# An attention layer in three-part float32: later column sums in the last image, a third form buffer and a shorter bias in the first, a reordered end

## The chip, the cores and the metric

The kernel runs on one core of one Trainium2 chip. The time is that of one execution of the whole program on the device, in microseconds (us). Before the change it was 2398.16 us, the median of three runs (2396.82 to 2399.83).

## The reference, cut to what matters

```python
# x: (4, 64, 64, 256); N = 64*64 = 4096, C = 256, C2 = 128
q = x @ Wq + bq          # (B, N, C2)
k = x @ Wk + bk          # (B, N, C2)
v = x @ Wv + bv          # (B, N, C)
pq, pk = q.reshape(B, C2, N), k.reshape(B, C2, N)
pv = v.reshape(B, C, N)
energy = einsum('bcn,bcm->bnm', pq, pk)      # 4096 x 4096 for each image
attention = softmax(energy, axis=-1)
out = einsum('bcm,bnm->bcn', pv, attention)  # 256 x 4096
result = gamma * out.reshape(x.shape) + x
```

Four images, each with its own 4096 by 4096 attention. The softmax is taken without subtracting a maximum; the kernel checks at its end that all sums lie in a safe range and has a second, general path behind a branch for the case that they do not.

## The kernel before, in words

Every float32 operand of a large product is split into forms: an upper part h, a lower part l and a third, d, which carries the correction, and each product is made of the three pairs. The forms are stored in the type that TensorE (PE) streams at one column per cycle. ScalarE (ACT) makes h, VectorE (DVE) makes l and d. So each large product is three matmuls on PE, one activation on ACT and two operations on DVE.

Work is staged like this:

- **Start** (lines 116 to 140 and 548 to 574). Weights and bias are loaded, Wq with Wk by the ACT queue, Wv by SyncE's. `weights(w)` scales a weight tile on ACT (line 160) and makes its forms with `split` (line 152 on ACT, 155 on DVE); w = 0 is q and k together, w = 1 is v. The bias of q and k is split too: an upper form on ACT (line 560) and a lower on DVE (line 563), each over 128 rows at 1/128 of its value, since `biased` (line 243) adds them by products with a tile of ones. The first tile of x is transposed (line 198), split (`x_forms`, lines 209, 211, 213) and multiplied.
- **First image's projections** (loop at line 575, 16 iterations i). An iteration issues, on PE: the f = 0 and 1 products of q and k (`products(0, i, 0, (0, 1))`, eight matmuls, line 229), those of v (eight), then for i + 1 the f = 2 products of q and k (four), the bias (four), the f = 2 products of v (four), and the transposes for i + 2 (four, line 198). On ACT, in this order: the h form of q and k (line 268), the h form of v (line 152), `seed_qk` for i + 1 (line 251), the h form of x for i + 2 (line 209), `seed_v` for i + 1 (line 260, two). The seeds scale a PSUM bank in place between the f = 2 products and the others. On DVE: two forms of q and k (line 271), two of v (line 155), two of x (211, 213). `qk_forms` takes its tile f from a ring of two buffers (tag "pf"), and `store` (line 290) sends it to DRAM by four DMAs on GpSimd's (POOL's) queue: k and q, for each of two halves. Parts of the first two attention steps are laid into iterations 7 to 12, and `load_q` and `load_k` stand at iterations 4, 5, 6, 8 and 11 on POOL's queue, behind the stores.
- **Attention steps** (loop at line 613). 512 steps n: 128 per image, in groups of NU = 16; t = n % 16 is the place in a group. A group is 512 rows of queries, a step 256 keys. Step n issues `cross(n+2)` (two products, line 318, each then scaled by ACT, line 319, in its PSUM tile; there are two such tiles), `attend(n, 0)` (six products into banks a0 and b0, line 378), `energy(n+2)` (four products, line 333, and two exponentials on ACT, line 336), `attend(n, 1)` (six, into a1 and b1). `upper` makes h of the exponentials on ACT (line 342), `halves` adds them to the running sum on DVE (line 351) and makes l and d (356, 358); in a group's last step it also adds the two halves of the sum (line 362). In steps of the first three images the next image's projections are woven in; the last image has attention alone.
- **End of a group.** At t = 15 `emptied(n, 0)` copies banks a0 and b0 to the tile o (ACT, line 392; o has one buffer) and `sum_forms` splits the sum (lines 404, 406). `emptied(n, 1)` copies a1 and b1 at t = 0 of the next group in the first three images and at t = 1 in the last (`late`). In the same step, behind it on PE, `sums` multiplies the column sums with a tile of ones (z, line 416, two products) and copies one row of z on ACT (line 417). In the last image z takes a bank that the second copy of line 392 has just emptied. `finish` then runs one piece a step from that step on: sums to DRAM and back, reciprocal (429), sum of the two parts of o (432), reciprocals spread over all rows by DMA, product (438), an accumulating DMA of x on POOL's queue (442) and the store on SyncE's (446).
- **The last group's end** (`finish_last`, line 453): attend(n, 0); zp, eight small products for the sums (459); reciprocal (463); spread (466); the range check (450, 451, 473); the d products of attend(n, 1); rp, the reciprocals on all rows (478); the rest of attend(n, 1); np (481). ACT copies b1 (482), then r (484). DVE ends with lines 485 to 492, two stores leave (488, 493), and `again` (494) is written for the branch.

Nothing reorders the instructions: each engine runs them in the order in which the code issues them.

Of the kernel before, what the change touches and what calls it, by code (L numbers as in the profile page):

```python
# [9 lines left out]
F32 = mybir.dt.float32  # L10
# [10 lines left out]
def kernel(  # L21
# [79 lines left out]
    with ExitStack() as fast:  # L101
# [45 lines left out]
                if next(pieces, StopIteration) is StopIteration:  # L147
                    active.remove(pieces)

        def split(h, l, d, y, scale=E):  # L150

            nc.scalar.activation(h, y, AF.Identity, scale=UPPER * scale)
            yield
            for t, f in ((d, 1.0 / scale + 1.0), (l, 1.0 / scale)):
                nc.vector.scalar_tensor_tensor(t, h.bitcast(F32), -f, y, ALU.mult, ALU.add)
                yield

        def weights(w):

            nc.scalar.mul(scaled[:, w], raw[:, w], E ** -(w + 1))  # L160
            yield from split(*(wf[:, w, f] for f in range(3)), scaled[:, w])

        def image(b):
            for g in range(NG):
# [73 lines left out]
        def biased(i):  # L238

            to = units[0, 0, i]  # L240
            for f in range(2):
                for s in range(2):
                    nc.tensor.matmul(  # L243
                        to[:, s, :], ones_r, bf[:, f, :], start=False, stop=False,
                        skip_group_check=True,
                    )

        def seed_qk(b, i):
            y = units[0, b, i]
# [13 lines left out]

        def qk_forms(b, i):
            y = units.pop((0, b, i))
            f = work.tile([P, 2, 3, C], F32R, tag="pf", name=f"f_{b}_{i}")
            h = f[:, :, 0, :]
            nc.scalar.activation(h, y, AF.Identity, scale=UPPER / 64)
            yield
            for j, s, op in ((1, -64.0, ALU.add), (2, 64.0 * (1.0 + E), ALU.subtract)):  # L270
                nc.vector.scalar_tensor_tensor(f[:, :, j, :], h.bitcast(F32), s, y, ALU.mult, op)  # L271
                yield
            for s in range(2):
                stores.append((kf[b, i // 2 + NU // 2 * s][:, i % 2], f[:, s, :, C2:]))
                stores.append((qd[b, i // NJ + NG // 2 * s][:, i % NJ], f[:, s, :, :C2]))
# [69 lines left out]
        def halves(n):  # L345
            if n >= B * STEPS:
                return
            x, h = units[n]
            if n % NU:
                s = now["s"]  # L350
                nc.vector.tensor_tensor(s, s, x, ALU.add)  # L351
            else:
                now["s"] = x
            ld = ppool.tile([P, 2, 2, NB], F32R, tag="ld", name=f"ld_{n}")
            l, d = ld[:, 0], ld[:, 1]
            nc.vector.tensor_tensor(l, x, h.bitcast(F32), ALU.subtract)  # L356

            nc.vector.scalar_tensor_tensor(  # L358
                d, h.bitcast(F32), 1.0 + E, x, ALU.mult, ALU.subtract
            )  # L360
            if n % NU == NU - 1:
                nc.vector.tensor_tensor(s[:, 0, :], s[:, 0, :], s[:, 1, :], ALU.add)
                now["sum"] = s
            units[n] = h, l, d

        def attend(n, j, order=(0, 1, 2)):
# [20 lines left out]
        def emptied(n, j, banks=None):  # L387

            if j == 0:
                now["o"] = work.tile([P, 2, 2, NB], F32, tag="o", name=f"o_{n // NU}", bufs=1)  # L390
            for c, scale in enumerate((gam2, gam1)):
                nc.scalar.activation(  # L392
                    now["o"][:, c, j, :],
                    banks[c] if banks else now["ab"[c], j],
                    AF.Identity,
                    scale=scale,
                )
# [55 lines left out]
        def finish_last(n, xr):  # L453

            b, g = B - 1, NG - 1
            attend(n, 0)
            zp = ps_e.tile([P, NJ], F32, tag="e", name="zp")
            for j in range(NJ):
                nc.tensor.matmul(
                    zp[:, j : j + 1], now["sum"][:, 0, j::NJ], ones[:, :1], start=True, stop=True  # L460
                )
            r4 = rall[:, B * NG - 1, :]
            nc.vector.reciprocal(r4, zp)
            work_ = ppool.tile([P, 2, NB], F32, tag="x", name="last")
            spread, ok = work_[:, 0].rearrange("p (q j) -> p q j", j=NJ), work_[:, 1, : B * NG * NJ]
            nc.vector.tensor_tensor(
                spread,
                ident.unsqueeze(2).to_broadcast([P, P, NJ]),
                r4.unsqueeze(1).to_broadcast([P, P, NJ]),
                ALU.mult,  # L470
            )
            inside(ok, rall.rearrange("p n j -> p (n j)"))
            nc.vector.tensor_reduce(zs, ok, AX.X, ALU.min)
            emptied(n, 0)
            o = now["o"]
            attend(n, 1, (2,))
            rp = ps_e.tile([P, NB], F32, tag="e", name="rp")
            nc.tensor.matmul(rp, ones, work_[:, 0], start=True, stop=True)
            attend(n, 1, (0, 1))
            np_ = ps_p.tile([P, 1], F32, tag="p0", name="np")  # L480
            nc.tensor.matmul(np_, ones, zs, start=True, stop=True)
            nc.scalar.activation(o[:, 1, 1, :], now["b", 1], AF.Identity, scale=gam1)
            r = work.tile([P, NB], F32, tag="r", name="r_last", bufs=1)
            nc.scalar.copy(r, rp)
            nc.vector.tensor_tensor(o[:, 0, 0, :], o[:, 0, 0, :], o[:, 1, 0, :], ALU.add)
            nc.vector.tensor_tensor(o[:, 0, 0, :], o[:, 0, 0, :], r, ALU.mult)
            nc.vector.tensor_tensor(xr[:, 0, :], xr[:, 0, :], o[:, 0, 0, :], ALU.add)
            nc.sync.dma_start(og[b, g][:, 0], xr[:, 0, :])
            nc.vector.tensor_tensor(o[:, 1, 1, :], o[:, 1, 1, :], r, ALU.mult)
            nc.vector.tensor_tensor(xr[:, 1, :], xr[:, 1, :], o[:, 1, 1, :], ALU.add)  # L490
            nc.vector.scalar_tensor_tensor(o[:, 0, 1, :], now["a", 1], gam2, r, ALU.mult, ALU.mult)
            nc.vector.tensor_tensor(xr[:, 1, :], xr[:, 1, :], o[:, 0, 1, :], ALU.add)
            nc.sync.dma_start(og[b, g][:, 1], xr[:, 1, :])
            nc.vector.tensor_scalar(again, np_, P - 0.5, None, ALU.is_lt)


        R = STEPS // NI
# [51 lines left out]
        now["turn"], now["banks"] = 0, [(ps_p, "p0"), (ps_p, "p1")]  # L549
        rings = cycle(now["banks"]), cycle([(ps_o, tag) for tag in ("a0", "a1", "b0", "b1")])  # L550
        image(0)
        for i in range(4):
            load_x(0, i)
        bf = work.tile([P, 3, KC, 2, P], F32R, tag="xf", name="bf", bufs=1)
        bf = bf[:, 0].rearrange("p k s a -> p k (s a)")
        transposed(0, 0)
        first = [weights(0), x_forms(0, 0), weights(1)]
        for pieces in first + first:
            next(pieces)
        nc.scalar.activation(bf[:, 0], bias, AF.Identity, scale=UPPER / P)  # L560
        for pieces in first:
            next(pieces)
        nc.vector.scalar_tensor_tensor(
            bf[:, 1], bias, 1.0 / P, bf[:, 0].bitcast(F32), ALU.mult, ALU.subtract
        )
        nc.gpsimd.tensor_scalar(bias, bias, REST, None, ALU.mult)
        products(0, 0, 0, (2,))
        products(0, 0, 1, (2,))
# [6 lines left out]
        for i in range(NI):  # L575
            products(0, i, 0, (0, 1))
            qk = qk_forms(0, i)
            next(qk)
            products(0, i, 1, (0, 1))
            vs = v_forms(0, i)  # L580
            next(vs)
            xs = iter(())
            if i + 1 < NI:
                products(0, i + 1, 0, (2,))
                biased(i + 1)
                seed_qk(0, i + 1)
                products(0, i + 1, 1, (2,))
            if i + 2 < NI:
                transposed(0, i + 2)
                xs = x_forms(0, i + 2)  # L590
                next(xs)
            if i + 1 < NI:
                seed_v(0, i + 1)
            load_x(0, i + 4)
            for pieces in (qk, vs, xs):
                for _ in pieces:
                    pass
            store()
            if i in (7, 10):
                cross(i // 9)  # L600
            elif i in (8, 11):
                energy(i // 9)
            elif i in (9, 12):
                upper(i // 10)
            elif i == 14:
                halves(0)
            if i == 4:
                load_q(0, 0)
            if i in (4, 5, 6):
                load_k(i - 4)  # L610
            elif i in (8, 11):
                load_k(3 + i // 9)
        for n in range(B * STEPS):
# [33 lines left out]
            else:  # L647
                upper(n + LOOK)
            step(p, "pe")
            if t == late and n > 1:  # L650
                sums(n - 1 - late)
                active.append(finish(n // NU - 1, now["o"], now["total"]))
            halves(n + 1)
            if turn:
# [232 lines left out]
```

## Time and profile before

| | |
|---|---|
| time, median of 3 runs | 2398.16 us (2396.82 to 2399.83) |
| profiled execution, its own time | 2397.88 us |
| its span | 2396.1 us |
| granted TensorE clock over the span | 0.996 |
| PE busy | 2355.5 us (98%), 11158 matmuls |
| DVE busy | 2135.3 us (89%) |
| ACT busy | 1882.2 us (79%) |
| POOL busy | 580.7 us (24%) |
| attention products (lines 318, 333, 378) on the chain that ended last | 87% |

A busy PE is the mean of overlapping records: a 512-column product lasts 0.39 us in its record but the next starts 0.227 us after it. In the timeline a row gives the start, the length, engine, line and operation, what is written and read, and in brackets how long the engine had been idle and what released it. Where several instructions of a group follow each other they are merged into one row with a count.

### The profile page before, as it was taken

To read this page: it belongs to the slowest core of one execution; us is meant where nothing else is said; L and a number is where in the kernel's file an instruction comes from. 1 tells how busy PE (TensorE), PEld (TensorE's weight loads), DVE (VectorE), ACT (ScalarE), POOL (GpSimd) and SP (SyncE) were. 2 spreads that over 40 slices of the span, in tenths; PEclk is the share of its full clock that TensorE was granted. 3 is DMA by queue.
4 is the path that set the end of the run, shared out by engine and by line. 5 is a ranking of instruction groups with operands and counts; after the bars stand their busy time and mean duration, and the time that the engine had idled before them with its cause. 6 is when DMAs were issued, how large, how long until landed. Compare 5 with 4: busy or idle time off the path is not lost.

```text
span 2396.1 us, 31995 instructions
## 1 busy us (share of the span) xinstructions
PE 2355.5 (98%) x11158; PEld 1967.6 (82%) x11158; DVE 2135.3 (89%) x2111; ACT 1882.2 (79%) x3093; POOL 580.7 (24%) x943
## 2 busy tenths in 40 slices
PE   8999999999999999999999999999999999999998
PEld 7888888888888888888888888888888787777776
DVE  6889999999999999999999999999998888888887
ACT  6777788887888887888877888878887777777775
POOL 5422222222322222222232222222223111111110
PEclk9999999999999999999999999999999999999999
DMA  9857666567896576566697665676669545445443
GB/s 216 177 139 199 169 165 171 144 174 183 262 274 163 147 187 178 157 166 156 164 342 220 159 175 142 175 188 156 167 175 337 134 128 128 126 111 129 114 124 88
DMA packets 243991, 413.83 MB, mean 173 GB/s; under 512 B 26031, under 2 KB 141487, under 8 KB 243822
## 3 DMA queue, kind: packets, MB, share of 16 engines
q0 software_dynamic: 203152, 368.77, 59.2%
q1 hardware_dynamic: 40126, 42.67, 5.7%
q8 instruction: 91, 1.49, 0.3%
q14 instruction: 78, 0.64, 0.1%
q10 hardware_dynamic: 544, 0.26, 0.0%
HBM read 306.64 MB, written 104.98 MB: 172 GB/s over the span
## 4 chain that ended last, share of the span: by engine, by line
PE 96%; ACT 2%; DVE 1%; DMA 1%; issue 0%; POOL 0%; SPq 0%; ACTq 0%; DVEq 0%
PE a L378 39%; PE b L378 19%; PE e L333 19%; PE e L318 10%; PE qv L229 7%; PE xt L198 1%; PE z L416 1%; ACT x L336 0%; ACT o L392 0%; DMA qd<-f 0%; ACT qv L260 0%; DMA raw<-in_L_conv_Wv_dram 0%; PE qv L243 0%; ACT xf L209 0%; DVE ld L358 0%
## 5 line engine op out<-in xcount | busy, mean ns | idle before, releaser
L336 ACT ACTIVATE x<-e 128x512 f32<-128x512 f32 x960 | 522.0, 596 | 301.7 <-PE e L333 295.4
L305 POOL DMA_DIRECT2D k<-kf x512 | 275.5, 538 | 1738.3 <-PE e L333 1678.3
L356 DVE TENSOR_TENSOR ld<-x,h 128x1024 fp32r<-128x1024 f32 x480 | 586.0, 1221 | 100.5 <-ACT h L342 55.8
L351 DVE TENSOR_TENSOR s<-s,x 128x1024 f32<-128x1024 f32 x480 | 586.5, 1222 | 99.7 <-ACT x L336 97.5
L378 PE MATMUL a<-h,v 128*128 128x512 f32 x2048 | 642.9, 395 | 0.0
L319 ACT ACTIVATE e<-e 128x512 f32<-128x512 f32 x1024 | 546.4, 572 | 119.7 <-PE e L318 119.3
L378 PE MATMUL b<-ld,v 128*128 128x512 f32 x2048 | 632.7, 390 | 1.7 <-DVE f L271 1.5
L378 PE MATMUL a<-ld,v 128*128 128x512 f32 x2048 | 633.8, 391 | 0.0
L358 DVE SCALAR_TENSOR_TENSOR ld<-h,x 128x1024 fp32r<-128x1024 f32 x480 | 584.7, 1218 | 0.0
L333 PE MATMUL e<-q,k 128*128 128x512 f32 x2048 | 547.7, 389 | 0.0
L342 ACT ACTIVATE h<-x 128x1024 fp32r<-128x1024 f32 x480 | 510.5, 1064 | 13.2
L378 PEld LDWEIGHTS b<-ld,v 128*128 128x128 f32 x2048 | 384.8, 188 | 84.6 <-issue 1.9
L378 PEld LDWEIGHTS a<-ld,v 128*128 128x128 f32 x2048 | 385.4, 188 | 83.4
L333 PEld LDWEIGHTS e<-q,k 128*128 128x128 f32 x2048 | 384.2, 188 | 79.7
L378 PEld LDWEIGHTS a<-h,v 128*128 128x128 f32 x2048 | 369.5, 189 | 70.6 <-ACT o L392 7.3
L318 PE MATMUL e<-q,k 128*128 128x512 f32 x1024 | 316.2, 390 | 0.0
L318 PEld LDWEIGHTS e<-q,k 128*128 128x128 f32 x1024 | 192.2, 188 | 40.8
L229 PEld LDWEIGHTS qv<-xf,wf 128*128 128x128 f32 x768 | 107.5, 191 | 17.9 <-ACT qv L260 8.0
L229 PE MATMUL qv<-xf,wf 128*128 128x256 f32 x768 | 114.5, 285 | 7.2 <-ACT qv L260 5.4
L229 PE MATMUL qv<-wf,xf 128*128 128x256 f32 x768 | 114.9, 286 | 3.6 <-DVE xf L211 1.9
L229 PEld LDWEIGHTS qv<-wf,xf 128*128 128x128 f32 x768 | 108.1, 192 | 12.7 <-ACT qv L251 2.6
L290 POOL DMA_DIRECT2D kf<-f x128 | 98.3, 768 | 29.1 <-DVE f L271 6.9
(84 smaller groups left out, 1230.4 us busy)
## 6 DMA issues: line engine op xcount, KB each, us to landing
k<-kf POOLq DMA_DIRECT2D x512, 384.0 KB, 3.6
vf<-vf POOLq DMA_DIRECT2D x48, 768.0 KB, 5.3
v<-vf POOLq DMA_DIRECT2D x48, 768.0 KB, 8.3
kf<-f POOLq DMA_DIRECT2D x128, 192.0 KB, 4.4
qd<-f POOLq DMA_DIRECT2D x128, 192.0 KB, 4.4
q<-qd POOLq DMA_DIRECT2D x32, 768.0 KB, 5.2
o<-in_x_dram POOLq DMA_DIRECT2D x31, 512.0 KB, 7.4
out_dram<-o SPq DMA_DIRECT2D x31, 512.0 KB
```

Of the source, the lines that this page charges most:

```text
L229: nc.tensor.matmul(to[:, s, :], left, right.rearrange("p s a -> p (s a)") if w else right, start=(f == 2 and s == k == 0), stop=(f == 1 an ...
L290: nc.gpsimd.dma_start(to, f)
L305: nc.gpsimd.dma_start(t, kf[b, u % NU])
L318: nc.tensor.matmul(e, *forms(n, i, 2), start=True, stop=False, skip_group_check=True)
L319: nc.scalar.mul(e, e, -REST)
L333: nc.tensor.matmul(e, *forms(n, i, f), start=False, stop=(f == 1), skip_group_check=True)
L336: nc.scalar.activation(x[:, i, :], e, AF.Exp, scale=(1.0 + E) ** 3 / E)
L342: nc.scalar.activation(h, units[n], AF.Identity, scale=UPPER)
L351: nc.vector.tensor_tensor(s, s, x, ALU.add)
L356: nc.vector.tensor_tensor(l, x, h.bitcast(F32), ALU.subtract)
L358: nc.vector.scalar_tensor_tensor(d, h.bitcast(F32), 1.0 + E, x, ALU.mult, ALU.subtract)
L378: nc.tensor.matmul(to, vall[:, t, f, i, j * P : (j + 1) * P], units[n][f][:, i, :], start=(t == 0 and i == 0 and f != 1), stop=(t == NU - ...
```

## The change

Five edits.

1. **Last image's column sums.** `sums` and the start of `finish` move from t = 1 to t = 2 in the last image (`t == 2 * late`); `emptied` stays. In the first three images (late = 0) nothing moves.
2. **Third buffer.** Every third `qk_forms` tile of the first image is a fixed tile f3, in a buffer of the q ring (tag "q", two buffers) that `load_q` does not use yet.
3. **seed_v earlier.** In the first image's loop `seed_v(0, i + 1)` is issued ahead of the transposes and the h form of x for i + 2. The order on ACT becomes h of q and k, h of v, seed_qk, seed_v (two), h of x.
4. **Bias and weights.** The bias is one product for each half, over 64 rows: a zero tile whose row 0 holds the upper form and row 32 the lower. `biased` issues two matmuls in place of four. The weights' scaling moves from ACT to DVE, and their h form reads the unscaled weights. In program order DVE gets the zero fill and both scalings ahead of all forms, and two one-row bias operations in place of one over 128 rows.
5. **The end.** In the last step the halves of the sum are added ahead of l and d. `finish_last` issues zp and the range check ahead of attend(n, 0), then rp and np, then all of attend(n, 1). ACT copies r ahead of b1. `again` is written ahead of the last products, and the second half is done in three DVE operations in place of four.

```diff
-        def split(h, l, d, y, scale=E):
+        def split(h, l, d, y):
...
         def weights(w):
-            nc.scalar.mul(scaled[:, w], raw[:, w], E ** -(w + 1))
-            yield from split(*(wf[:, w, f] for f in range(3)), scaled[:, w])
+            y, c = scaled[:, w], E ** -(w + 1)
+            nc.vector.tensor_scalar(y, raw[:, w], c, None, ALU.mult)
+            h, l, d = (wf[:, w, f] for f in range(3))
+            nc.scalar.activation(h, raw[:, w], AF.Identity, scale=UPPER * E * c)
+            yield
+            for t, f in ((d, 1.0 / E + 1.0), (l, 1.0 / E)):
+                nc.vector.scalar_tensor_tensor(t, h.bitcast(F32), -f, y, ALU.mult, ALU.add)
+                yield
...
         def biased(i):
-            for f in range(2):
-                for s in range(2):
-                    nc.tensor.matmul(
-                        to[:, s, :], ones_r, bf[:, f, :], start=False, stop=False,
-                        skip_group_check=True,
-                    )
+            for s in range(2):
+                nc.tensor.matmul(
+                    to[:, s, :], ones_r[:64], bf[:64], start=False, stop=False,
+                    skip_group_check=True,
+                )
...
         def qk_forms(b, i):
-            f = work.tile([P, 2, 3, C], F32R, tag="pf", name=f"f_{b}_{i}")
+            if b == 0 and i % 3 == 2:
+                f = f3
+            else:
+                f = work.tile([P, 2, 3, C], F32R, tag="pf", name=f"f_{b}_{i}")
...
         def halves(n):
+            def whole():
+                nc.vector.tensor_tensor(s[:, 0, :], s[:, 0, :], s[:, 1, :], ALU.add)
+                now["sum"] = s
+
+            if n == B * STEPS - 1:
+                whole()
...
-            if n % NU == NU - 1:
-                nc.vector.tensor_tensor(s[:, 0, :], s[:, 0, :], s[:, 1, :], ALU.add)
-                now["sum"] = s
+            if n % NU == NU - 1 and n < B * STEPS - 1:
+                whole()
...
         def finish_last(n, xr):
-            attend(n, 0)
             zp = ps_e.tile([P, NJ], F32, tag="e", name="zp")
...
             nc.vector.tensor_reduce(zs, ok, AX.X, ALU.min)
+            attend(n, 0)
             emptied(n, 0)
             o = now["o"]
-            attend(n, 1, (2,))
             rp = ps_e.tile([P, NB], F32, tag="e", name="rp")
             nc.tensor.matmul(rp, ones, work_[:, 0], start=True, stop=True)
-            attend(n, 1, (0, 1))
             np_ = ps_p.tile([P, 1], F32, tag="p0", name="np")
             nc.tensor.matmul(np_, ones, zs, start=True, stop=True)
-            nc.scalar.activation(o[:, 1, 1, :], now["b", 1], AF.Identity, scale=gam1)
+            attend(n, 1, (2, 0, 1))
             r = work.tile([P, NB], F32, tag="r", name="r_last", bufs=1)
             nc.scalar.copy(r, rp)
+            nc.scalar.activation(o[:, 1, 1, :], now["b", 1], AF.Identity, scale=gam1)
             nc.vector.tensor_tensor(o[:, 0, 0, :], o[:, 0, 0, :], o[:, 1, 0, :], ALU.add)
+            nc.vector.tensor_scalar(again, np_, P - 0.5, None, ALU.is_lt)
...
-            nc.vector.tensor_tensor(o[:, 1, 1, :], o[:, 1, 1, :], r, ALU.mult)
-            nc.vector.tensor_tensor(xr[:, 1, :], xr[:, 1, :], o[:, 1, 1, :], ALU.add)
-            nc.vector.scalar_tensor_tensor(o[:, 0, 1, :], now["a", 1], gam2, r, ALU.mult, ALU.mult)
-            nc.vector.tensor_tensor(xr[:, 1, :], xr[:, 1, :], o[:, 0, 1, :], ALU.add)
+            y = o[:, 1, 1, :]
+            nc.vector.scalar_tensor_tensor(y, now["a", 1], gam2, y, ALU.mult, ALU.add)
+            nc.vector.tensor_tensor(y, y, r, ALU.mult)
+            nc.vector.tensor_tensor(xr[:, 1, :], xr[:, 1, :], y, ALU.add)
             nc.sync.dma_start(og[b, g][:, 1], xr[:, 1, :])
-            nc.vector.tensor_scalar(again, np_, P - 0.5, None, ALU.is_lt)
...
         image(0)
+        f3 = work.tile([P, 2, 3, C], F32R, tag="q", name="f3")
...
-        bf = bf[:, 0].rearrange("p k s a -> p k (s a)")
+        bf, bh = (bf[:, 0, k].rearrange("p s a -> p (s a)") for k in range(KC))
+        nc.vector.tensor_scalar(bf[:64], zs[:64].to_broadcast([64, C]), 0.0, None, ALU.mult)
         transposed(0, 0)
...
-        nc.scalar.activation(bf[:, 0], bias, AF.Identity, scale=UPPER / P)
+        nc.scalar.activation(bh[:64], bias[:64], AF.Identity, scale=UPPER)
         for pieces in first:
             next(pieces)
-        nc.vector.scalar_tensor_tensor(
-            bf[:, 1], bias, 1.0 / P, bf[:, 0].bitcast(F32), ALU.mult, ALU.subtract
-        )
+        nc.vector.tensor_copy(bf[:1], bh[:1].bitcast(F32))
+        nc.vector.tensor_tensor(bf[32:33], bias[32:33], bh[32:33].bitcast(F32), ALU.subtract)
...
                 products(0, i + 1, 1, (2,))
+                seed_v(0, i + 1)
             if i + 2 < NI:
                 transposed(0, i + 2)
                 xs = x_forms(0, i + 2)
                 next(xs)
-            if i + 1 < NI:
-                seed_v(0, i + 1)
...
-            if t == late and n > 1:
-                sums(n - 1 - late)
+            if t == 2 * late and n > 2:
+                sums(n - 1 - 2 * late)
                 active.append(finish(n // NU - 1, now["o"], now["total"]))
```

More of the change, by code (lines that the diff above doesn't have):

```diff
@@ L148, in proceed @@
                     active.remove(pieces)
-        def split(h, l, d, y, scale=E):
-            nc.scalar.activation(h, y, AF.Identity, scale=UPPER * scale)
+        def split(h, l, d, y):
+            nc.scalar.activation(h, y, AF.Identity, scale=UPPER * E)
             yield
-            for t, f in ((d, 1.0 / scale + 1.0), (l, 1.0 / scale)):
+            for t, f in ((d, 1.0 / E + 1.0), (l, 1.0 / E)):
                 nc.vector.scalar_tensor_tensor(t, h.bitcast(F32), -f, y, ALU.mult, ALU.add)
@@ L158, in weights @@
         def weights(w):
-            nc.scalar.mul(scaled[:, w], raw[:, w], E ** -(w + 1))
-            yield from split(*(wf[:, w, f] for f in range(3)), scaled[:, w])
+            y, c = scaled[:, w], E ** -(w + 1)
[3 more added lines that the diff above has]
+            yield
+            for t, f in ((d, 1.0 / E + 1.0), (l, 1.0 / E)):
+                nc.vector.scalar_tensor_tensor(t, h.bitcast(F32), -f, y, ALU.mult, ALU.add)
+                yield
         def image(b):
```

## The prediction

> **What bounds the kernel now.** I read the page's chain of work first: 96% of it is PE, so time goes only where PE stops, runs slowly, or has not started. I then asked for the waits of PE over the whole span (columns: who waited for whom, us in total, times, longest).
>
> ```profile
> PE z L416 <- ACT o L392: 15.0, 8, 1.9
> PE qv L229 <- ACT qv L260: 5.4, 10, 0.5
> PE qv L229 <- ACT qv L251: 1.8, 2, 1.6
> ```
>
> The column sums of the last image (z) wait eight times, 1.9 us each; the first image's projections wait some 7 us. Between them, the attention steps of the first three images show no wait worth a line and the change leaves their order as it is. So three places count: first image, last image, tail.
>
> The timeline of one z wait (start, length in us, engine, line):
>
> ```profile
> 1911.93 1.07 PE L333 MATMUL e<-q,k 128*128 128x512 f32 x4
> 1913.56 0.69 ACT L392 ACTIVATE o<-a,gam 128x512 f32<-128x512 f32 x1
> 1914.13 0.70 ACT L392 ACTIVATE o<-b,gam 128x512 f32<-128x512 f32 x1
> 1914.70 1.08 ACT L342 ACTIVATE h<-x 128x1024 fp32r<-128x1024 f32 x1
> 1914.88 0.73 PE L416 MATMUL z<-zf,ones 128*128 128x512 f32 x2 [1.88 <-ACT o L392]
> ```
>
> PE issues a 512-column product every 0.227 us, so after the four of L333 the next slot is 1912.84. z starts at 1914.88 because its bank is emptied by the second copy (L392), which ends at 1914.83. A step is 18 such products, 4.08 us; a group of 16 steps and a z is 65.73 us. The groups in the windows below take 67.88, so a wait costs **2.15 us**. Two groups take 69.52. In both, z and the products behind it ran at half clock (columns ahead of the clock: busy us and counts of PE, PEld, DVE, ACT, POOL):
>
> ```profile
> 1845.60:1849.01 3.41, 3.41 (x9) 2.63 (x9) 0.43 (x1) 1.23 (x2) 0.00 (x0) 0.50 0.89 321
> 1980.48:2048.36 67.88, 66.00 (x291) 54.35 (x290) 58.19 (x53) 52.95 (x86) 10.13 (x18) 1.00 0.49 125
> 2116.25:2185.77 69.52, 67.64 (x291) 55.49 (x290) 58.19 (x53) 53.09 (x86) 10.13 (x18) 0.98 0.47 121
> ```
>
> **Last image: −17.7 us.** z, its one-row copy and the finish behind it move from t = 1 to t = 2; the copies (L392) stay at t = 1, so at t = 2 the bank has been free for a step and z costs its 0.45 us alone. What is late next is ACT: after the copies it still has h(n+2) (to 1915.70), then the two scalings of the next cross products (L319, 0.55 us apart), which PE needs at once. PE would issue attend(n,1) 1912.84 to 1914.20, cross to 1914.66, attend(n+1,0) to 1916.02; its L333 needs the first scaled tile, ready at 1916.27, and the second at 1916.80. That is 0.28 + 0.07 = 0.35 us of new wait. The z copy (0.57) no longer stands ahead of L319. DVE's order moves the reciprocal, the o sum and the o product by a step, at the same cost. So 8 × (2.15 − 0.35) = 14.4, and the two half-clock stretches, 69.52 − 67.88 = 1.64 each, go with the waits: 3.3. Bounds: new wait 0 gives 20.5; 1.0 us of it, and the half clock staying, give 9.2.
>
> The half clock: eight waits of one length, two followed by it, none elsewhere in the steps. The Trainium skill (TensorE: Matmul & The Clock Gate, "Why this matters for your kernels") warns only of idle gaps over about 3 us. By that rule a 1.9 us gap could not cause it and 3.3 us would stay; the trace speaks against the rule, as both stretches begin at the z behind such a gap.
>
> **First image: −10.6 us.** PE waits in an iteration, from the timeline:
>
> ```profile
> 27.57 1.22 PE L229 MATMUL qv<-wf,xf 128*128 128x256 f32 x8
> 27.85 0.60 ACT L209 ACTIVATE xf<-xt 128x512 fp32r<-128x512 f32 x1 [0.33 <-PE xt L198]
> 28.35 0.93 ACT L260 ACTIVATE qv<-qv,bvs 128x256 f32<-128x256 f32 x2
> 28.48 0.69 DVE L211 SCALAR_TENSOR_TENSOR xf<-xf,xt 128x512 fp32r<-128x512 f32 x1 [0.48 <-ACT xf L209]
> 29.32 1.21 PE L229 MATMUL qv<-xf,wf 128*128 128x256 f32 x8 [0.54 <-ACT qv L260]
> ```
>
> A plain iteration takes 4.59 us (22.98 to 27.57 to 32.16). Two things hold it there. The v products wait for L260, queued behind the xf form. And f has two buffers: the form is started by ACT at 24.89, the last of its four stores is issued at 29.65, and such a store landed about 4.5 us after issue where ACT waited for it (20.41 to 24.87); a buffer is thus held 9.2 us, 4.6 for each of two. ACT's waits from 15 to 90 us say the same:
>
> ```profile
> ACT f L268 <- DMA qd<-f: 5.1, 4, 3.5
> ```
>
> With three buffers, 9.2 / 3 = 3.1 us no longer binds. Call the start of the next image part's f = 2 products 0. Products are 0.117 us apart: four, then two bias products instead of four (0.48 to 0.71), four for v (0.71), the transposes (1.19). ACT: seed_qk at 0.92 (0.44 after the bias products start), seed_v at 1.41, 0.85 long to the next slot, xf at 2.26 to 2.86; DVE's d form 2.89 to 3.58; the next f = 2 products at 3.62. PE fits inside: eight from 1.55, eight from 2.49, free at 3.43. DVE's six operations at 0.60 fill 3.6; POOL's four stores at 0.78, 3.1. So 3.62, and I take **3.65**. The DMA must then carry 4 × 192 + 256 KB in 3.65 us, 288 GB/s, where 40 to 57 us moved 316.
>
> From the first q products at 13.44 to those of iteration 15 at 84.90 is 71.46 us. Then: the first interval 4.95 less the 0.24 of two bias products and little more, 4.6; eight plain ones 29.2; the six that carry parts of steps 0 and 1 cost 4.0 with a cross or an h (ACT, 0.98 more, against its slack) and 4.35 with an energy (PE, 3.42 + 0.91), 24.7. The load of q and three of k at iterations 4 to 6 (1.97 MB, at the 360 GB/s that 48 to 54 us reached 5.5 us of queue) held f for 1.2 and 3.5 us before; each iteration then has 3.65 − 2.9 = 0.75 spare and the third buffer 1.6, so I keep 2.3 us of it. Sum 60.8. Bounds: 68 if every interval is held by the DMA, 58 with no stall.
>
> **Start: +0.6 us.**
>
> ```profile
> 8.43 0.63 ACT L152 ACTIVATE wf<-scaled 128x512 fp32r<-128x512 f32 x1
> 9.09 1.29 DVE L155 SCALAR_TENSOR_TENSOR wf<-wf,scaled 128x512 fp32r<-128x512 f32 x2 [1.85 <-ACT wf L152]
> 11.97 0.79 PE L243 MATMUL qv<-bf,ones 128*128 128x256 f32 x2 [0.49 <-DVE bf L563]
> 12.80 0.58 ACT L251 ACTIVATE qv<-qv 128x512 f32<-128x512 f32 x1 [3.44 <-PE qv L243]
> ```
>
> The end of the start is the bias: DVE, then PE at 11.97, ACT at 12.80, the q products at 13.44. ACT loses a scaling, but both scalings now stand at the head of DVE's queue, and the second waits for Wv, which landed at 7.76 (when ACT's scaling of it began). Behind it stand the d forms of wf and xf that ran at 5.95 and 6.56 before. So DVE does the scaling (a plain scalar product on 512 columns is not in the trace: 0.22 for 128, 0.69 for two tensors; I take 0.6), six forms at 0.6 and two bias rows of 0.3 to 0.4 where one took 0.42: 7.76 + 0.6 + 3.6 + 0.65 = 12.6 against 11.97. Bounds 0.2 and 1.0. The zero fill and both smaller forms hide in DVE's idle time ahead of 4.6 us.
>
> **Tail: −3.2 us.**
>
> ```profile
> 2381.61 2.07 PE L478 MATMUL rp<-last,ones 128*128 128x512 f32 x2 [0.43 <-DVE last L466]
> 2383.72 0.59 ACT L484 COPY r_last<-rp 128x512 f32<-128x512 f32 x1 [1.82 <-PE rp L478]
> 2387.78 0.69 DVE L492 TENSOR_TENSOR xr<-xr,o 128x512 f32<-128x512 f32 x1
> 2388.39 0.15 DVE L494 TENSOR_SCALAR again<-np 128x1 int32<-128x1 f32 x1
> ```
>
> zp moves ahead of attend(n,0): six products of 0.227 earlier, 2377.22; its sum is ready since DVE now adds the halves first. The d form that this delays by 0.69 is needed only after zp, which hides it. rp then starts behind attend(n,0) at 2380.42, 1.19 earlier. From r's copy to the end DVE has five operations of 0.69 and again (0.15) where it had six: 0.54 less. Together 1.7. again is written some 5 us earlier; all engines read it to branch, and 7.56 us lie between its end and the span's. The sequencers' records, which the views leave out, show POOL's drain behind the branch ending about 1.5 us after SyncE's, so I add 1.5. Bounds: 0.7 (nothing for again, a slower rp) and 4.5 (rp at full clock, 1 us less).
>
> **Sum.** The profiled execution took 2397.88 (span 2396.1, 1.8 around it), against a median of 2398.16, so nothing is rescaled. 2397.88 + 0.6 − 10.6 − 17.7 − 3.2 = **2367.0**.
>
> **Rivals.**
> - The DMA becomes the first image's bound: stores of 512-byte pieces queue up, and f waits three buffers deep. For it: the DMA is at nine tenths in the page's first slice. Against: 316 GB/s over 40 to 57. First image 68 instead of 60.8: 2374. Chance 0.15.
> - A new ACT wait takes z's place: 1.0 instead of 0.35 us for each group, 5.2 us: 2372. For it: ACT has 3.3 us of extra work in three steps with 0.93 idle each. Chance 0.10.
> - The half clock is not the wait's doing and comes as often: +3.3, 2370. Chance 0.06.
> - Slower: the one o buffer. The read that adds x into o now leaves POOL a step later, so the store leaves at 1960.8 in place of 1956.72, 12.5 us ahead of the next group's copies (1973.28). It decides from a store over 12.5 us; to lose 31 us in eight groups it would have to take 16.4. The read of the same size landed in 7.6. Over 2398: chance 0.02. That the sums do not move is excluded by the order of both programs.
> - The forecast, 2360 to 2371: 0.67.
>
> Two rivals together give 2379. **Range** 2360 to 2377: low end from both end bounds (−2.8, −2.8, −1.3), high end past each rival alone. A difference of 0.2% (4.8 us) is about what a measurement here can tell from no change. Faster by more: 0.96, within: 0.02, slower: 0.02.
>
> **What would show it.** The wait of z on o gone, with 0.3 to 0.4 us before L333 at t = 2; groups of 66.1 us; no 0.50 clock in the last image's steps; plain iterations of 3.6 to 3.8 us with DVE full and no wait of f on its stores but behind the q load; q products starting near 14.0; rp 1.2 us earlier against the last attend. I am wrong if iterations stay over 4.2 us, or if PE waits elsewhere at t = 2.

## The result, and the profile after

The changed kernel takes **2369.84 us** (median of four runs, 2369.02 to 2370.82) where the kernel before takes 2398.95 in the same comparison (four runs, 2396.82 to 2399.83): 1.2% less, ratio 0.988 with a 95% interval of 0.9863 to 0.9897. The forecast was 2367.0 in a range of 2360 to 2377. The profiled execution took 2370.2 us, with a span of 2368.4, 27.7 less than before.

Where these 27.7 us lie, from the starts of the same products in both traces:

| stretch | before | after | difference | forecast |
|---|---|---|---|---|
| span's start to the first q products | 13.44 | 14.40 | +0.96 | +0.6 |
| to the q products of iteration 15 | 71.46 | 64.19 | −7.27 | −10.6 |
| to the first group's z | 77.74 | 77.35 | −0.39 | 0 |
| steps of images 0 to 2, to the last z in image 2 (ahead of its last group) | 1605.75 | 1605.73 | 0.0 | 0 |
| that group and the last image, to the last energy product | 604.75 | 588.03 | −16.7 | −17.7 |
| tail | 22.96 | 18.73 | −4.2 | −3.2 |

**Last image.** First the waits of PE over the whole span, as before (who waited for whom, us in total, times, longest), its first and third line, then one line of PEld, the weight loads:

```profile
PE qv L235 <- DVE xf L217: 4.3, 1, 4.3
PE b L391 <- DVE f L279: 1.1, 1, 1.1
```

```profile
PEld e L341 <- ACT e L327: 6.0, 16, 0.6
```

The eight waits of z on the copies are gone, and so are those of the first image's products on seed_v. (The 4.3 us lie in the start, from 5.56 to 9.86 us.) In their place the weight loads of the energy products (L341) wait for ACT's scalings (L327), 16 times, twice a group. The timeline of the step with z shows how:

```profile
1970.86 1.08 ACT L350 ACTIVATE h<-x 128x1024 fp32r<-128x1024 f32 x1
1971.81 1.09 ACT L327 ACTIVATE e<-e 128x512 f32<-128x512 f32 x2
1972.47 0.30 PEld L341 LDWEIGHTS e<-q,k 128*128 128x128 f32 x2 [0.56 <-ACT e L327]
1972.95 0.30 PEld L341 LDWEIGHTS e<-q,k 128*128 128x128 f32 x2 [0.18 <-ACT e L327]
1973.53 0.62 PE L429 MATMUL z<-zf,ones 128*128 128x512 f32 x2
```

z starts 0.23 us behind the last product of L341, with no idle time. The h form that the forecast named as late (here 1970.86 to 1971.94) holds back the two scalings. Of PE's four energy products the first starts 0.29 us late and the later ones 0.18 more: 0.47 us a group, where 0.35 was forecast. A group from z to z (busy us and counts of PE, PEld, DVE, ACT, POOL, then the granted clock):

```profile
1973.53:2039.73 66.20, 66.06 (x292) 54.27 (x291) 58.27 (x53) 52.87 (x87) 10.14 (x18) 1.00 0.47 128
```

All seven groups between the last image's first z and its last take 66.2, none at half clock.

**First image.** One iteration's f = 2 products, in the rows of PE; DVE's d form ahead of them:

```profile
24.85 0.69 DVE L217 SCALAR_TENSOR_TENSOR xf<-xf,xt 128x512 fp32r<-128x512 f32 x1 [0.41 <-ACT xf L215]
...
25.59 0.74 PE L235 MATMUL qv<-wf,xf 128*128 128x256 f32 x4
26.26 0.50 PE L248 MATMUL qv<-bf,ones 64*128 64x256 f32 x2
26.70 0.74 PE L235 MATMUL qv<-xf,wf 128*128 128x256 f32 x4
27.28 0.60 PE L204 MATMUL xt<-ident,xs 128*128 128x128 f32 x4
```

From the f = 2 products of q and k to the bias are 0.67 us, over the two bias products 0.44, to the transposes 0.58: 1.69 in all, where the forecast had 0.48, 0.23 and 0.48. The next f = 2 products start at 29.69, so a plain iteration takes **4.10** and not 3.65. f no longer waits in it. ACT's waits for stores from 15 to 90 us, which were 5.1 us before:

```profile
ACT f L276 <- DMA qd<-f: 1.1, 2, 0.6
```

**Start.** The scaling of Wv on DVE, and the two bias rows:

```profile
8.18 0.43 DVE L161 TENSOR_SCALAR scaled<-raw 128x512 f32<-128x512 f32 x1 [2.94 <-DMA raw<-in_L_conv_Wv_dram]
...
12.14 0.27 DVE L577 CAST bf<-bf 1x256 fp32r<-1x256 f32 x1
12.44 0.41 DVE L578 TENSOR_TENSOR bf<-bias,bf 1x256 fp32r<-1x256 f32 x1
```

Wv landed at 8.18 here and at 7.76 before, so 0.42 of the 0.96 us is its load. From its landing to the first q products it is 6.22 us here and 5.68 before, that is 0.54 more.

**Tail.** rp, r's copy, `again`, the last DVE operation:

```profile
2357.14 1.02 PE L490 MATMUL rp<-last,ones 128*128 128x512 f32 x2
2358.20 0.59 ACT L495 COPY r_last<-rp 128x512 f32<-128x512 f32 x1
2358.78 0.15 DVE L498 TENSOR_SCALAR again<-np 128x1 int32<-128x1 f32 x1
2361.80 0.69 DVE L505 TENSOR_TENSOR xr<-xr,o 128x512 f32<-128x512 f32 x1
```

DVE's last sum ends 12.80 us behind the start of the last energy product, 2349.69 (15.34 before), and the span 5.93 after that (7.62 before): −2.5 and −1.7. rp runs at full clock, 1.02 us in place of 2.07.

### The profile page after: what moved, and what is told of

It reads as the page before. It is cut to its first block, busy times and chain, and to the rows that moved or that the text cites. A ratio compares the mean times of both kernels' runs of the same rounds, so it can differ in the third digit from the quotient of the medians.

```text
span 2368.4 us, 31941 instructions
## 1 busy us (share of the span) xinstructions
PE 2350.2 (99%) x11126; PEld 1961.1 (83%) x11126; DVE 2135.9 (90%) x2114; ACT 1880.9 (79%) x3091; POOL 580.5 (25%) x943
## 4 chain that ended last, share of the span: by engine, by line
PE 97%; ACT 1%; DVE 1%; issue 0%; DMA 0%; SPq 0%; DVEq 0%; ACTq 0%
PE a L391 39%; PE e L341 20%; PE b L391 19%; PE e L326 10%; PE qv L235 8%; PE xt L204 1%; PE z L429 1%; ACT o L405 0%; ACT x L344 0%; PE qv L248 0%; DMA raw<-in_L_conv_Wv_dram 0%; ACT e L327 0%; ACT h L350 0%; DVE ld L372 0%; DVE f L279 0%
## 5 line engine op out<-in xcount | busy, mean ns | idle before, releaser
L327 ACT ACTIVATE e<-e 128x512 f32<-128x512 f32 x1024 | 546.6, 573 | 109.0 <-PE e L326 108.7
L341 PE MATMUL e<-q,k 128*128 128x512 f32 x2048 | 548.8, 390 | 1.1
L341 PEld LDWEIGHTS e<-q,k 128*128 128x128 f32 x2048 | 383.0, 188 | 84.4 <-ACT e L327 6.0
```

Of the source, the lines that this page charges most:

```text
L327: nc.scalar.mul(e, e, -REST)
L341: nc.tensor.matmul(e, *forms(n, i, f), start=False, stop=(f == 1), skip_group_check=True)
```

## The experiments

The theory after the result: the gains come in all four places, and the missing 2.8 us lie in the sizes of the forecast's terms. The largest is the bias product over 64 rows, which breaks PE's rhythm each time the row count changes; one mechanism, the buffers', was in part another than forecast. Most runs alter one thing in the changed kernel, two alter two and one alters three; times are medians of four runs each, and "before" on the same chips was 2397.09 to 2397.76. The intervals of the ratios are some 4 us wide to each side, so smaller differences between two runs are read from the stages in their traces.

**The bias over 128 rows.** The zero tile is filled over all rows, and the product reads all of it: the same two matmuls, no change of row count.

```diff
-                    to[:, s, :], ones_r[:64], bf[:64], start=False, stop=False,
+                    to[:, s, :], ones_r, bf, start=False, stop=False,
...
-        nc.vector.tensor_scalar(bf[:64], zs[:64].to_broadcast([64, C]), 0.0, None, ALU.mult)
+        nc.vector.tensor_scalar(bf, zs.to_broadcast([P, C]), 0.0, None, ALU.mult)
```

> The changed kernel with its bias product over all 128 rows (a zero tile of 128 rows, the same two rows filled) instead of 64. Theory: a product over 64 rows between products over 128 breaks the overlap of weight load and product, at each change of rows and between the two of them, 0.38 us an iteration in all, and it lies on the loop from the f = 2 products to the next ones. Then the f = 2 products to the bias take 0.57, the bias 0.24, the v products 0.48, a plain iteration 3.7 us instead of 4.09, and the time falls by 15 x 0.38 = 5.7 to 2364. Rival 1: the loads are exposed only because PE waits for the d form each time; then the distances at the bias stay and the iteration stays 4.09, 2370. Rival 2: the stores or DVE hold the iteration next, at 3.9 to 4.0: 2367 to 2368.

Measured: 2367.24 us (2366.71 to 2367.77), ratio 0.9873 (0.9857 to 0.989). The same rows of an iteration:

```profile
24.88 0.74 PE L235 MATMUL qv<-wf,xf 128*128 128x256 f32 x4
25.46 0.39 PE L248 MATMUL qv<-bf,ones 128*128 128x256 f32 x2
25.69 0.64 PE L235 MATMUL qv<-xf,wf 128*128 128x256 f32 x4
26.16 0.60 PE L204 MATMUL xt<-ident,xs 128*128 128x128 f32 x4
```

Now 0.58, 0.23 and 0.47, 1.28 in all in place of 1.69, and the plain iterations behind the first take 3.72 to 3.73. So it was the rows that held the iteration at 4.09, and not PE's wait for DVE's form or the stores. The single records tell why. Over 64 rows the products start at 25.93, 26.06, then 26.26 and 26.49 (the bias), then 26.70, 26.92, 27.04; over 128 rows each starts 0.12 after the one before. At both changes of the row count (26.26 and 26.70) the product's record begins with its own weight load and lasts 0.39 us in place of 0.28, as where a product has waited for DVE; elsewhere the load begins a product earlier. So the load isn't drawn ahead over such a change, and each change costs some 0.2. The Trainium skill (TensorE: Matmul & The Clock Gate, "LDWEIGHTS (loading the stationary operand)") says that a weight load's time goes by its columns and not its rows. The records agree, 183 and 186 ns over 64 rows and 186 to 193 over 128; the cost is not in the load's length but in when it may start.

The 0.41 us lie on a loop: f = 2 products, bias, those of v, transposes, ACT's seeds and xf, DVE's d form, the next f = 2 products. So they lengthen the iteration by 0.37. The whole first image gains less, 61.07 in place of 64.19: with shorter iterations the one that holds the load of q takes 5.23 (4.64 in the changed kernel), and f's waits on its stores are 1.9 us. This is the stall that the forecast had put at 2.3. So the time fell by 2.6 us, with 5.7 expected.

**Sums at t = 1 again** (edit 1 undone).

```diff
-            if t == 2 * late and n > 2:
-                sums(n - 1 - 2 * late)
+            if t == late and n > 1:
+                sums(n - 1 - late)
```

> The changed kernel with its column sums back at t = 1 in the last image (edit 1 undone alone). Theory: the eight waits of 1.9 us come back and the new ones of L327 go, 67.88 against 66.20 us for a group, 8 x 1.68 = 13.4, and some of the waits are followed by a stretch at half clock, 1.64 each, so 2383 to 2390, with at least one such stretch in the last image. Rival: the half clock has nothing to do with the waits; then none in the last image, as in the changed kernel, and 2383.

Measured: 2387.46 us (2385.29 to 2389.86), ratio 0.9954 (0.9937 to 0.997), 17.6 us over the changed kernel. The wait is back, to the digit, and with it half-clock stretches of 3.41 us from 1840.91, 2045.71 and 2318.78 on. First the wait, then one of the stretches as a row of the windows:

```profile
PE z L429 <- ACT o L405: 15.0, 8, 1.9
```

```profile
2045.70:2049.11 3.41, 3.41 (x9) 2.69 (x9) 0.41 (x2) 1.20 (x2) 0.00 (x0) 0.50 0.27 93
```

Each begins 0.1 to 0.8 us after the start of a z that waited. Of 16 such waits in this run and the kernel before, five were followed by half clock; the last images without them, in the changed kernel and in the other nine experiments, had none ahead of the tail. So the half clock follows the wait, though not each time. Which waits it follows can be read from the traces. The clock changes only at instants that lie whole multiples of 3.413 us apart: the three starts above are 204.80 and 273.07 apart, 60 and 80 times that. Cut at these instants, the time around two of the waits looks so:

```profile
1837.50:1840.91 3.41, 1.53 (x8) 0.94 (x7) 3.27 (x3) 3.11 (x6) 1.05 (x2) 1.00 0.96 313
1974.04:1977.45 3.41, 1.60 (x8) 0.99 (x6) 3.41 (x4) 2.48 (x6) 0.53 (x1) 1.00 0.28 80
```

In the first piece PE's whole gap of 1.88 us lies, and half clock follows at its end; in the second only 1.81 of it, the rest behind the cut, and none follows. It is so for all 16: in the five cases with half clock the gap lies whole in one piece, in the other eleven it is split and no piece holds more than 1.81. So the number of stretches depends on where the waits fall against these instants, and differs between runs: two in the kernel before, three here.

The rule of about 3 us that the forecast weighed (the Trainium skill, TensorE: Matmul & The Clock Gate, "Why this matters for your kernels") doesn't cover this: PE's gap here is 1.88 us, that of its weight loads 2.30.

**h behind the scalings.** In the last image the h form of step n+2 is not issued at t = 1, but in the next step, behind the two scalings of the cross products.

```diff
             cross(n + LOOK)
...
-            if t == 0 and n:
+            late = n >= (B - 1) * STEPS
+            if t in (0, 2 * late) and n > 2:
                 upper(n + LOOK - 1)
...
-            else:
+            elif not late or t != 1:
                 upper(n + LOOK)
```

> The changed kernel with one more move: in the last image h of unit n+2 is not made at t = 1 behind the copies, but at t = 2 behind the two scalings L327, as the code does after t = 15. Theory: a group still loses 66.20 - 65.73 = 0.47 us to PE's wait for those scalings, which stand behind h on ACT; with h behind them that wait goes, 8 x 0.47 = 3.8, time 2366, groups 65.7 us. Rival: l and d on DVE then come too late and PE waits for ld in its place: groups stay at 66.2 or more, 2370.

Measured: 2367.61 us (2366.73 to 2368.29), ratio 0.9874 (0.9857 to 0.989). A group, and the two ACT rows in their new order:

```profile
1972.26:2038.07 65.81, 65.81 (x291) 54.45 (x290) 58.00 (x53) 52.81 (x87) 10.14 (x18) 1.00 0.49 129
```

```profile
1970.03 1.10 ACT L327 ACTIVATE e<-e 128x512 f32<-128x512 f32 x2
1971.02 1.09 ACT L350 ACTIVATE h<-x 128x1024 fp32r<-128x1024 f32 x1
```

65.81 where 16 steps and a z alone make 65.73; PE is busy for all of it, and the table's last image, with the group ahead of it, takes 584.89 in place of 588.03. The new wait was h standing ahead of the scalings, and l and d, which come later for it, hold nothing up. In the traces this stretch is 3.1 us shorter; the median of the time fell by 2.2, with 3.8 expected.

**Two buffers** (edit 2 undone).

```diff
-            if b == 0 and i % 3 == 2:
+            if False:
                 f = f3
```

> The changed kernel without the third buffer (all forms of q and k from the ring of two). Theory: a buffer is held 9.2 us, so a plain iteration takes 4.6 us, f waits for its stores in most of them, and the q load costs its 3 to 5 us again: first image 71 to 74 us instead of 64.2, time 2377 to 2380. Rival: seed_v's place was what held the iteration, and the buffers bind only behind the q load: iterations stay 4.1, 2371 to 2374.

Measured: 2377.37 us (2376.15 to 2378.38), ratio 0.9913 (0.9897 to 0.993), 7.5 over the changed kernel. First q products to iteration 15: 70.92. ACT's waits from 15 to 90 us:

```profile
ACT f L276 <- DMA qd<-f: 10.2, 5, 4.9
```

But the six plain iterations behind the first take 4.09 to 4.16 and once 5.16, a mean of 4.30. Most of the time is lost at the load of q (7.82 and 6.39 us, where the changed kernel takes 4.64 and 4.85); part of the second is half clock, from 54.89 to 58.30, behind a gap of PE of 3.0 us. A buffer held 9.2 us, as the forecast had it, would have given 4.6 in each plain iteration. So the hold was too long in the forecast, and the cost of the 64 rows hides some of what is left of it.

**seed_v late** (edit 3 undone).

```diff
                 products(0, i + 1, 1, (2,))
-                seed_v(0, i + 1)
             if i + 2 < NI:
                 transposed(0, i + 2)
                 xs = x_forms(0, i + 2)
                 next(xs)
+            if i + 1 < NI:
+                seed_v(0, i + 1)
```

> The changed kernel with seed_v back behind the h form of x (edit 3 undone alone). Theory: the v products wait for seed_v again; with bias and buffers as changed the q products start 2.03 after the f = 2 ones, seed_v ends at 3.7, the v products run to 4.7, so a plain iteration takes 4.6 to 4.7 us and the time is 2377 to 2380. Rival: the two buffers alone held the iteration before; then it stays at 4.1 to 4.2 and the time at 2370 to 2372.

Measured: 2376.91 us (2376.16 to 2378.35), ratio 0.9912 (0.9895 to 0.9928). Plain iterations 4.74, 72.40 to iteration 15. PE's waits from 15 to 90 us:

```profile
PE qv L235 <- ACT qv L265: 5.6, 10, 0.6
```

That is the wait of the kernel before (5.4, ten times), and the iteration is 0.15 longer than its 4.59. So the rival, that two buffers alone held the iteration before, falls. With either edit undone, and the bias over 64 rows, the first image takes about as long as before (70.92 and 72.40 beside 71.46): the wait for seed_v lengthens every plain iteration, the two buffers mostly those at the load of q, and the two edits gain only together.

**Two buffers and the bias over 128 rows.** Both edits above in one kernel, to see the hold without the bias in front of it.

> The changed kernel with the bias products over 128 rows, and without the third buffer for the forms of q and k. In the prediction a buffer is held 9.2 us, so two of them bind an iteration at 4.6. The run with two buffers and the bias over 64 rows showed plain iterations of 4.09 to 4.16, so a hold of at most some 8.2 us, and lost its time at the load of q. My theory now: the hold is 8 to 8.3, so without the bias's cost the buffers bind at 4.0 to 4.15 (not 3.72), ACT shows waits of f on its stores in plain iterations, and the load of q costs some 4.3 us as there: A0 to A15 69 to 71, time 2375 to 2378. Rival A, the prediction as it stands: 4.6 in plain iterations, A0 to A15 73 to 75, 2379 to 2382. Rival B, the buffers bind at the load of q alone: plain iterations 3.72, A0 to A15 65 to 66, 2371 to 2373.

Measured: 2376.31 us (2375.22 to 2378.22), ratio 0.9909 (0.9893 to 0.9926); 69.76 to iteration 15. The iterations behind the first take 3.73, 4.94, 3.78, 3.72, 4.82, 3.78, a mean of 4.13, and then 8.17 and 6.08 at the load of q (the second again partly at half clock, from 52.95 to 56.37). f's waits on stores are 12.3 us in seven. The mean is what was expected, the even spacing isn't. The first buffer was held 10.49 us (16.37 to 26.86), the next ones 8.75 (21.09 to 29.84), 7.24 (26.86 to 34.10), 9.34 (29.84 to 39.18) and 8.33 us (34.10 to 42.43), a mean of 8.4 without the first, whose iteration ran partly at half clock: the last store of a tile landed 2.4 to 3.9 us after its issue, and in the first iteration 5.6.

**The old tail** (edit 5 undone). The edit is the diff of edit 5 read backwards.

> The changed kernel with edit 5 undone alone (the sum's halves added last, the end as before). From the last energy product to the span's end the changed kernel takes 18.73 us and the one before 22.96. Theory: the whole of edit 5 is that difference, 4.2 us, so 2374. Rival: part of it came from the steps ahead; then less.

Measured: 2375.43 us (2373.31 to 2375.84), ratio 0.9904 (0.9887 to 0.992). The tail takes 22.73, 4.0 more, and rp runs 1.88 us, at half clock from 2359.35. Of the 4.95 us between the two profiled spans the rest lies in the first image, which took 1.5 us more, 65.7, while the start took 0.6 less: more half clock in its first interval (5.69 for 5.04) and a longer stall at the load of q (5.42 for 4.64), both of which differ between runs.

**again written last.** Only this line is put back behind the last product of the changed kernel's tail.

> The changed kernel with again written last, behind the last sum, as before. Theory: from the last DVE operation to the span's end the changed kernel takes 5.9 us and the one before 7.6, since the engines read again and branch while DVE still works; with again last the 1.7 come back, less the 0.15 us that again no longer stands in the chain: 1.5 us more, 2371.3. Rival: the end hangs on the last store's landing; then again's place costs nothing and the time is 0.1 less.

Measured: 2372.44 us (2371.98 to 2373.53), ratio 0.9895 (0.9878 to 0.9911). The tail takes 20.39 in place of 18.73: 1.66 us for an operation of 0.15. Up to DVE's last sum the two tails are equal (12.80 us); from there to the end of the span it is 7.58 us here and 5.93 in the changed kernel. In the other runs it is 5.55 to 5.93 with `again` early, once 6.76, and 7.58 and 7.62 with `again` last, so the place of `again` is worth 0.8 to 2.1 us. The rival, that the last store alone sets the end, falls. The median rose by 2.6, with 1.5 expected.

**Scaling on ACT, bias over 128 rows.** The weights' part of edit 4 undone, on top of the first experiment.

```diff
-            y, c = scaled[:, w], E ** -(w + 1)
-            nc.vector.tensor_scalar(y, raw[:, w], c, None, ALU.mult)
-            h, l, d = (wf[:, w, f] for f in range(3))
-            nc.scalar.activation(h, raw[:, w], AF.Identity, scale=UPPER * E * c)
...
+            y = scaled[:, w]
+            nc.scalar.mul(y, raw[:, w], E ** -(w + 1))
+            yield from split(*(wf[:, w, f] for f in range(3)), y)
```

> The kernel with the bias over 128 rows, and the weights' scaling back on ACT. Theory: the second scaling no longer holds DVE until Wv has landed, the d forms run in that time, and the bias rows are ready 0.6 to 0.9 us earlier counted from Wv's landing: the q products start 5.2 to 5.5 us behind that landing and the time is 0.6 to 0.9 less than with the bias over 128 rows alone. Rival: ACT's extra 0.63 us between the landing and h eats it; no difference.

Measured: 2367.36 us (2366.26 to 2368.0), ratio 0.9872 (0.9855 to 0.9888), as in the first experiment, where 0.6 to 0.9 less was expected. From Wv's landing to the first q products it takes 6.01, against 6.19 there and 5.68 before the change. So the scaling on DVE costs 0.18 more than on ACT, whose two operations then stand ahead of DVE's forms; about 0.26 more are the two bias rows (0.27 + 0.41 where one operation took 0.42).

**Both repairs** (the bias over 128 rows with the scaling on ACT, and h behind the scalings).

> The changed kernel with both things that the earlier runs found: the bias products over 128 rows (and the weights' scaling back on ACT), and in the last image the upper form of step n+2 issued at t = 2 behind the scalings of the cross products in place of ahead of them. My theory is that the two losses lie in different stages and add: against the changed kernel plain iterations of 3.72 in place of 4.09 (A0 to A15 some 3.1 shorter in sum) and groups of 65.81 in place of 66.20 in the last image (8 x 0.39 = 3.1 shorter): 2369.8 - 2.5 - 2.3 (what the two runs apart gained in time) = 2365.0, between 2364 and 2366. Rival: the gains do not add, because the first image's gain only moves a wait to the start of the steps that follow: 2367.4 as in either run alone.

Measured: **2364.21 us** (2363.66 to 2365.57), ratio 0.9859 (0.9843 to 0.9875), 5.6 less than the changed kernel. Plain iterations 3.72, groups 65.81, the last image 584.89. The two gains, 2.6 and 2.2 us alone, add.

## Why the forecast was right, and where it was off

- **Last image (−17.7, measured −16.7): right.** The waits and both half-clock stretches went; undoing the edit brings back 17.6 us. That there were two such stretches to lose was luck. The whole difference is the new wait, 0.47 for 0.35: eight groups make 0.96. Its place and cause (h ahead of the scalings) were as forecast.
- **First image (−10.6, measured −7.3): mechanism right, one term too small.** The step that failed is "then two bias products instead of four (0.48 to 0.71)", costed at the 0.117 us of any other product. Over 64 rows they cost 0.41 us more than that, on the loop that sets the iteration. Of the excess over 60.8, 3.3 lie in the eight plain iterations (32.5 for 29.2), 1.9 in the six mixed ones (26.6 for 24.7), 0.4 in the first; 2.3 come back since the stall at the load of q did not show. With 128 rows the sizes come close: 3.72 for 3.65, 61.07 for 60.8, stall included.
- **The two causes that were to hold the plain iteration at 4.59: one right, one not.** Both edits were needed for the gain, as the forecast said, but the buffers did not hold the plain iterations before the change. The forecast's landing of 4.5 us is that of the first iteration's store. The tile it reckons with, started at 24.89, was free when its last store, issued at 29.65, landed at 32.92: 8.0 us and not 9.2, where two iterations take 9.2. So seed_v alone held 4.59. The buffers bind once seed_v is early: with holds of 7.2 to 9.3 (a mean of 8.4 over 128 rows) two of them allow about 4.2, and most of their cost falls on the load of q.
- **Start (+0.6, measured +0.96): right but for the load.** 0.54 of it belongs to the edit, 0.42 to Wv's landing, which came between 7.54 and 9.20 in the runs. The scaling took 0.43 where 0.6 was assumed, and the bias rows 0.68 for 0.65.
- **Tail (−3.2, measured −4.2): right, its named upper term came true.** rp at full clock is the 1 us that was kept as a bound. For `again` 1.5 was taken; 1.7 was measured between these two traces.
- **Rivals.** The DMA as a bound: no, f waits 1.1 us in all. A new ACT wait of 1.0: no, 0.47. The half clock apart from the waits: no. The one o buffer: nothing of it in the waits.

What stays open: why the buffers' hold varies by 2 us between tiles. That the old four bias products over 128 rows would now do better than two over 64 (3.72 + 0.23 = 3.95 for 4.09) is only worked out; it wasn't tried.

## What to carry to other kernels

A product that is made smaller in rows isn't cheaper if its neighbours have another row count: padding it with zeros to the neighbours' shape was worth 0.37 us in each iteration here. Where an engine's wait is removed, look at the order of the queue that released it; the next wait was the same engine's next two operations, and putting them ahead of one that nobody needed yet took it away. And where either of two causes alone is enough to keep a stretch as long as it was, undoing one edit at a time shows each at the full gain; here 7.5 and 7.1 us of 7.3.

## What the runs showed of the hardware that was not expected

- Where products over 64 rows stand between products over 128, the weight load isn't drawn ahead over the change: some 0.2 us at each change, 0.41 for the two of an iteration, where two more products over 128 rows cost 0.23.
- The clock changed only at instants 3.413 us apart, or whole multiples of that. After the start, half clock came where one such piece held at least 1.88 us of a gap of PE (five z waits, and 2.33 and 3.22 us in the two runs with two buffers), and not where it held up to 1.81. At rp in the old tail it came behind a gap of 0.43 us, after 2.8 us that held zp's eight one-column products and only two of 512 columns.
- In the start, products of 256 columns stood 0.213 us apart, as at half clock, until 16.1 to 18.9 us in every run. So of the first interval 1.9 to 4.8 us ran so, and it took 4.7 to 6.0 us.
- A one-tensor scalar product on 512 float32 columns took 0.43 us on DVE, and one of two tensors 0.69. The Trainium skill (VectorE: DVE Perf Modes, "Mode 2×_2P — use both read ports for one tensor") puts the first at two elements a cycle and the second at one; the records agree in direction, 1.6 times and not 2.
- `again`, 0.15 us of DVE work, was worth 1.66 us by its place between two traces of otherwise equal tails: in the records all engines read it and branch before they end.
